# Two of ten row pairs are turned by VectorE after a trip over DRAM instead of by TensorE

## The chip, the cores and the metric

The program runs on one core of one Trainium2 chip. A core has five engines, each with its own in-order list of instructions: TensorE (PE in the profile, matmuls; PEld its weight loads), VectorE (DVE), ScalarE (ACT), GpSimd (POOL) and SyncE (SP, which here only issues transfers). Transfers run on 16 DMA engines. The metric is the device time of one execution in microseconds (us), lower is better; the median of several executions is given.

## The reference

One layer of graph attention over 2708 nodes with 1024 features, fp32, with a residual:

```python
h = jnp.maximum(_layernorm(x, axis=-1), 0.0)
q = h @ W_q.T + b_q
k = h @ W_k.T + b_k
v = h @ W_v.T + b_v
z = (1.0 / math.sqrt(1024)) * (q @ k.T)
spare_z = z * adj
spare_z = jnp.where(spare_z == 0.0, -10000.0, spare_z)
out = jax.nn.softmax(spare_z, axis=1) @ v
x = x + jnp.maximum(out, 0.0)
```

`adj` is a 0/1 matrix with a density of 0.15%, about four neighbours per row. x and adj are made by the seed; the weights are 1024x1024.

## The kernel before, in words

**What it computes.** The rows are sorted by their number of neighbours and cut into 22 tiles of 128. The scores of a row are products of one row of a transformed q with a few rows of h, and the result is a weighted sum of a few rows of h times the value weights; so there are two large products with a 1024x1024 matrix: the q products (h times a matrix made from W_q and W_k) and the o products (weighted rows times W_v). Between them lies the attention: for each tile, neighbours' rows of h are gathered, multiplied with the q row and summed (`junk<-g,pq`, L863), exponentiated (`w<-zall`, L872, on ScalarE), normed (L906 to L911) and added up with weights (`u<-g,coef`, L912 on ScalarE for the first neighbour, L923 on VectorE for the others).

**Units.** A unit is a pair of tiles. Units 0 to 9 are q pairs (tiles 0 and 1, 2 and 3, ...), units 10 to 18 are o pairs, and a single tile (`alone`) ends the program. Each unit is multiplied by a scheme with seven half-sized products instead of eight (`multiply` and `opened`): with a11, a12 the two halves of the first tile, a21, a22 of the second, s1 = a22 + a21, s3 = a11 - a21, s2 = s1 - a11 and s4 = a12 - s2. The products of unit n run on TensorE in the order s2, a12, s4, s3, then a11 and s1 of unit n+1, then a22 of unit n. Each is 8 records of 128x512 (L1011), in three PSUM banks (two named `ps`, one `psy`); ScalarE copies banks out (`u<-psy` L1060 after s2, `q<-ps` L1094 after a12, `taken<-psy` L1081 after s3, `psy<-ps` L1024 after a11, `p<-ps` L1029 after s1, `q<-psy` L1105 after a22) and fills new ones with the bias (`ps<-bp_sb` L760).

**Turning the rows.** TensorE wants its left operand with the features on the partitions. The rows of a q pair are gathered from `h_dram` into tiles named `qr` by GpSimd (L612). `half_turned` (L415) then makes 4 transposes of 128x128 on TensorE for each half tile into PSUM (`pt`; 8 records a half); ScalarE copies a11, a12 and a22 out (`a<-pt`, L718), and VectorE reads a21 from PSUM when it makes s1 and s3 (`put`, L722). Most o rows go another way: ScalarE writes a tile in an order of quarters (`v<-u`, L944), stores it to `u_dram`, SP reads it back with four transfers that put each quarter of the columns on its own 32 partitions (`by_quarters`, L700), and VectorE turns blocks of 32x32 (`faces`, L705), which then gives the same operand; `blocks` chooses by whether a tile is in `faced`.

**What sets the order.** In unit `FIRST` = 4 and after, VectorE's list is written by hand: the units' instructions come where the Python program emits them, and the attention runs as a stream (`attention`) that `advance(share)` moves on after each product by a number of microseconds of VectorE work. ScalarE, GpSimd, SP and TensorE are put in order by a scheduler that follows its own estimate of when each instruction's inputs are ready, with `issue_after` as a rule that one instruction comes after another in issue. The attention can start once the table of sorted neighbours has been written to DRAM by GpSimd (L626) and read back by SP (`tab`, L638 and L642). On ScalarE also stands `M<-M` (L1280), two halves that change the sign of a loaded part of W_v (t1, loaded at L1274 through SP), which the s1 products of the o units use.

## Time and profile before

| | us |
|---|---|
| median of 3 runs | 631.02 |
| lowest, highest | 630.44, 631.29 |
| profiled execution, whole | 627.16 |
| its span in the profile | 625.5 |
| TensorE busy | 618.3 (99%) |
| VectorE busy | 525.7 (84%) |
| ScalarE busy | 291.0 (47%) |
| GpSimd busy | 368.9 (59%) |

The profiled execution is one run; 1.66 us of it lie outside the span, and it is 3.86 us shorter than the median of the others. The granted TensorE clock is 0.997 of full speed. A row of a timeline has the start in us from the span's beginning, the duration, the engine, the line, the operation, the tiles (out<-in) and, in brackets, how long the engine stood idle before it and what ended that. A row of a group has the count, the busy time and the mean duration in ns. In a row of a stretch, each engine's busy time comes with its number of instructions, then the granted clock, the busy share of the DMA engines and GB/s.

### The profile page before, as it was taken

Reading aid. Unit: us, or ns where it says so; the run is one execution under the profiler, and the core shown is the slowest. Engines: PE = TensorE matmul, PEld = TensorE weight load, DVE = VectorE, ACT = ScalarE, POOL = GpSimd, SP = SyncE. Lnnn points to the kernel's source line nnn. Section 1 sums busy time; section 2 is a strip of 40 time slices with the busy share of each in tenths; the row PEclk is TensorE's granted clock in tenths of the full one; section 3 lists DMA queues with packets and bytes.
Section 4 is the critical chain, followed back from the end, with each engine's and each line's share of the span. In section 5 each row is a group of like instructions: output and inputs, shape, how many; then the busy total and the mean of one; then the engine's idle time right before and its main releaser. Section 6 shows DMA issues by size and latency. Waiting matters only on the chain.

```text
span 625.5 us, 6068 instructions
## 1 busy us (share of the span) xinstructions
PE 618.3 (99%) x1571; PEld 309.9 (50%) x1571; DVE 525.7 (84%) x1024; ACT 291.0 (47%) x421; POOL 368.9 (59%) x394
## 2 busy tenths in 40 slices
PE   9999999999999999999999999999999999999996
PEld 5777776444444444454444444444444444444442
DVE  5999878987988947979898999998988899898541
ACT  3538976749777373434331532443442433432300
POOL 2638870786668577856655343577577657752331
PEclk9999999999999999999999999999999999999998
DMA  8998898687797559997696999999999999995571
GB/s 336 407 374 318 332 352 326 211 273 292 267 370 277 175 180 364 342 347 233 218 362 170 397 340 313 339 326 320 328 328 320 333 306 338 288 301 144 137 266 71
DMA packets 65808, 183.24 MB, mean 293 GB/s; under 512 B 10039, under 2 KB 20615, under 8 KB 65128
## 3 DMA queue, kind: packets, MB, share of 16 engines
q0 software_dynamic: 26656, 86.02, 43.7%
q1 hardware_dynamic: 32170, 72.06, 33.0%
q10 hardware_dynamic: 6942, 24.73, 10.1%
q8 instruction: 14, 0.23, 0.1%
q14 instruction: 26, 0.21, 0.1%
HBM read 147.23 MB, written 43.88 MB: 306 GB/s over the span
## 4 chain that ended last, share of the span: by engine, by line
PE 90%; DMA 3%; POOL 2%; ACT 2%; DVE 1%; issue 0%; POOLq 0%; ACTq 0%
PE ps L1011 42%; PE psy L1011 30%; PE ps_y L476 7%; PE ps_x L476 4%; PE ps_z L476 4%; PE pt L415 2%; POOL hsum L298 2%; DMA x<-in_x_dram 2%; ACT sized L368 1%; DMA wlow<-in_wq_dram 1%; DVE wlow L444 1%; DVE s L722 0%; ACT junk_x L246 0%; PE ps_h L1230 0%; PE ps_v L594 0%
## 5 line engine op out<-in xcount | busy, mean ns | idle before, releaser
L610 POOL DMA_INDIRECT g<-h_dram,tab x93 | 120.5, 1296 | 62.4 <-issue 19.4
L1011 PE MATMUL psy<-wlow,s 128*128 128x512 f32 x320 | 144.0, 593 | 0.2 <-ACT u L1060 0.2
L1011 PE MATMUL ps<-M,a 128*128 128x512 f32 x320 | 144.1, 593 | 0.1
L863 DVE SCALAR_TENSOR_TENSOR junk<-g,pq 128x1024 uint8<-128x1024 f32 x92 | 112.3, 1220 | 9.3 <-DMA g<-h_dram,tab 7.3
L1011 PE MATMUL ps<-M,s 128*128 128x512 f32 x240 | 107.9, 592 | 0.0
L1011 PEld LDWEIGHTS ps<-M,a 128*128 128x128 f32 x320 | 60.0, 190 | 72.6 <-issue 71.5
L1011 PEld LDWEIGHTS psy<-wlow,s 128*128 128x128 f32 x320 | 60.0, 190 | 72.5 <-issue 71.3
L923 DVE SCALAR_TENSOR_TENSOR u<-g,coef,u 128x1024 f32<-128x1024 f32 x70 | 89.8, 1282 | 7.2 <-ACT u L912 5.4
L389 DVE FIND_INDEX8 at<-ones,adj 128x8 uint32<-128x685 f32 (+1 forms) x88 | 74.4, 863 | 0.0
L1011 PEld LDWEIGHTS ps<-M,s 128*128 128x128 f32 x240 | 45.5, 190 | 57.2 <-issue 55.5
L1011 PE MATMUL psy<-wlow,a 128*128 128x512 f32 x160 | 71.9, 592 | 0.0
L368 ACT ACTIVATE sized<-adj 128x2708 uint8<-128x2708 f32 (+1 forms) x22 | 54.3, 2468 | 7.5 <-DMA adj<-in_adj_dram 6.2
L298 POOL TENSOR_TENSOR hsum<-hsum,x 128x256 f32<-128x256 f32 (+1 forms) x56 | 38.6, 725 | 24.9 <-DVE wlow L444 21.5
L1115 POOL DMA_INDIRECT y<-in_x_dram,tab x19 | 33.2, 1749 | 31.4 <-ACT y L1132 16.6
L1011 PEld LDWEIGHTS psy<-wlow,a 128*128 128x128 f32 x160 | 30.4, 190 | 38.3 <-issue 36.6
L808 POOL DMA_INDIRECT out_dram<-y,tab x21 | 27.9, 1329 | 15.8 <-issue 13.6
L1011 PE MATMUL ps<-wlow,s 128*128 128x512 f32 x80 | 36.0, 593 | 0.0
L944 ACT COPY v<-u 128x1024 f32<-128x1024 f32 x20 | 20.9, 1046 | 29.9 <-DVE u L923 27.6
L912 ACT ACTIVATE u<-g,coef 128x1024 f32<-128x1024 f32 x16 | 18.4, 1148 | 25.7 <-DVE coef L911 20.5
L626 POOL DMA_INDIRECT tab_dram<-tab,pos_i x22 | 21.6, 982 | 14.3 <-DVE pos_i L689 8.8
L276 ACT ACTIVATE x<-x,r 128x1024 f32<-128x1024 f32 (+1 forms) x22 | 25.9, 1235 | 6.9 <-POOL r L266 6.9
L760 ACT COPY ps<-bp_sb 128x512 f32<-128x512 f32 x42 | 24.6, 596 | 8.7 <-DVE y L1150 7.2
(253 smaller groups left out, 839.1 us busy)
## 6 DMA issues: line engine op xcount, KB each, us to landing
adj<-in_adj_dram SPq DMA_DIRECT2D x21, 1354.0 KB, 11.4
x<-in_x_dram SPq DMA_DIRECT2D x21, 512.0 KB, 7.7
h_dram<-x ACTq DMA_DIRECT2D x21, 512.0 KB, 7.9
u_dram<-v ACTq DMA_DIRECT2D x20, 512.0 KB, 8.2
or<-u_dram SPq DMA_DIRECT2D x80, 128.0 KB, 7.9
q_late<-q SPq DMA_DIRECT2D x12, 512.0 KB, 8.5
pq<-q_late POOLq DMA_DIRECT2D x12, 512.0 KB, 9.3
M<-in_wv_dram SPq DMA_DIRECT2D x3, 1024.0 KB
```

The source lines that it names most:

```text
L276: nc.scalar.activation(xs[i][:n], xs[i][:n], AF.Relu, bias=r[:n, 4, i:i + 1], scale=r[:n, 3, i:i + 1])
L298: small.append(nc.gpsimd.tensor_add(hsum[:n, cols], hsum[:n, cols], xt[:n, cols]))
L368: nc.scalar.activation(sized[:n], a[:n, :, :PW], AF.Abs, accum_out=total[:n, t:t + 1])
L389: nc.vector.max_index(at[:n, k - first_k, g, :], ones[:n, 0:8], a[:n, g, :])
L476: mm = nc.tensor.matmul(bank, a_tile(o + H * a[0], a[1], i), b(o), start=first and o == 0, stop=(o == H - 1), skip_group_check=True)
L610: return nc.gpsimd.indirect_dma_start(out=dst, out_offset=None, in_=src, in_offset=off, bounds_check=N - 1, oob_is_err=False)
L760: nc.scalar.copy(return_[h], row[:, h * NB:(h + 1) * NB])
L808: to = nc.gpsimd.indirect_dma_start(out=out, out_offset=bass.IndirectOffsetOnAxis(ap=ptab.bitcast(U32)[:n, t, SLOTS:SLOTS + 1], axis=0), i ...
L863: chained(lambda: nc.vector.scalar_tensor_tensor(junk, g_of[t][s], 1.0, tq[t], op0=ALU.mult, op1=ALU.mult, accum_out=zall[:, t, s:s + 1]))
L923: chained(lambda: nc.vector.scalar_tensor_tensor(u, g_of[t][s], coef[:, s:s + 1], u, op0=ALU.mult, op1=ALU.add))
L1011: mm = nc.tensor.matmul(bank, a[:, c, :], b[:, c, :], start=False, stop=(c == 3), skip_group_check=True)
L1115: return nc.gpsimd.indirect_dma_start(out=y[:n], out_offset=None, in_=x, in_offset=off, compute_op=ALU.add)
```

## The change

The units 5 and 6 (`ROUND`; tiles 10 to 13) take for their q rows the way of the o rows. `send_round` copies each gathered tile in the order of quarters on ScalarE into a tile `way` and stores it to a new array `r_dram` (512 KB a tile, issued by ScalarE); `come_round` reads it back with `by_quarters` (four reads of 128 KB a tile, on SP) into `came`; `faces` turns the halves on VectorE. Their transposes on TensorE and the copies out of PSUM go. Round about:

- the reload of the table comes on SP after the last read of `came`, and is written in unit 4 after product 0 rather than 4;
- the store of q tile 8 comes on SP after the reload of the table, and so does the load of t1, now written in unit 4 rather than 7;
- the rows of unit 6 are gathered in unit 3 (at 4), earlier than before;
- unit 5's a11 and a12 are written two products later, together with the rest of the pair;
- the attention stream gets 2.3/7 us less after each product of unit 5, and one and a half shares at its start, after the last product of unit 4.

```diff
@@ steps of the stream
             elif step[0] == "b":
-                reload(*halves[first])
+                with tc.issue_after(came[-1].ins):
+                    tabbed.append(reload(*halves[first]))
@@ steps_at
-... (4, 4): "b0"}
+... (4, 0): "b0"}
@@ opened
         if n == FIRST:
             follow("o0")
+            send_round(ROUND[0])
@@ between
+        if n == FIRST - 1:
+            for m in ROUND[1:]:
+                send_round(m)
+            come_round(ROUND[0])
@@ q_results
-            (nc.scalar if t < 4 else nc.sync).dma_start(dst, q)
+            with tc.issue_after(tabbed[-1].ins) if t == EARLY else nullcontext():
+                stored.append((nc.scalar if t < 4 else nc.sync).dma_start(dst, q))
@@ new functions
+    ROUND = range(FIRST + 1, FIRST + 1 + 2)
+    came, tabbed, stored = [], [], []
+    def in_quarters(v, u):
+        return nc.scalar.copy(v.rearrange("p (a c r) -> p c a r", a=QUADS, r=QP),
+                              u.rearrange("p (c a r) -> p c a r", a=QUADS, r=QP))
+    def round_row(n, k):
+        t = 2 * (n - ROUND[0]) + k
+        return r_dram[t * P:(t + 1) * P, :]
+    def send_round(n):
+        for k, xt in enumerate(rows_of[n]):
+            v = row_tile(f"way_{n}_{k}")
+            in_quarters(v, xt)
+            nc.scalar.dma_start(round_row(n, k), v)
+    def come_round(n):
+        rows_of[n] = [row_tile(f"came_{n}_{k}") for k in range(2)]
+        for k, xt in enumerate(rows_of[n]):
+            came.append(by_quarters(xt, round_row(n, k)))
@@ the loop over units
+        if n > FIRST and n + 1 in ROUND:
+            share -= 2.3 / 7
@@ after
-            for at, place, src in (((-2, 0), t1, of_wv(0, 0)), ((0, 3), b21, of_wv(1, 0))):
-                if (n - last_q, i) == at:
-                    nc.sync.dma_start(place, src)
+            if (n - last_q, i) == (0, 3):
+                nc.sync.dma_start(b21, of_wv(1, 0))
             elif (n, i) == (FIRST, 6):
-                advance(share)
+                advance(1.5 * share)
                 if i == (3 if n == 0 else 4 if turn else 0):
                     ops_of[n + 1] = blocks(...)
-                    with tc.issue_after(products[-1].ins) if n + 1 == FIRST else nullcontext():
-                        ops_of[n + 1][1]()
+                    if n + 1 != ROUND[0]:
+                        with tc.issue_after(products[-1].ins) if n + 1 == FIRST else nullcontext():
+                            ops_of[n + 1][1]()
+                if i == (4 if n == 0 else 5 if turn else 2):
+                    if n + 1 == ROUND[0]:
                         ops_of[n + 1][1]()
-                if i == (4 if n == 0 else 5 if turn else 2):
                     ops_of[n + 1][2]()
+            if (n, i) == (FIRST - 1, 4):
+                rows_of[FIRST + 2] = load_rows(units[FIRST + 2])
+            if (n, i) == (FIRST - 1, 6):
+                with tc.issue_after(stored[-1].ins):
+                    come_round(FIRST + 2)
+            if (n, i) == (FIRST, 0):
+                with tc.issue_after(tabbed[-1].ins):
+                    tabbed.append(nc.sync.dma_start(t1, of_wv(0, 0)))
```

What the scheduler makes of it is seen in the order of instructions on the engines. First ScalarE, from the negation of t1 on; before, the exponential of the first attention tile (`w_1661`) stood three rows behind it, and the copy of unit 5's a12 result (its bank is `ps_1592`) comes eight rows after the last one shown:

```order
L1280 ACTIVATE M<-M 128x1024 x2
L1081 COPY taken<-psy 128x512
L1024 COPY psy<-ps_1592 128x512
L872 ACTIVATE w_1661<-zall 128x3
L1029 COPY p_1643<-ps_1594 128x512
L912 ACTIVATE u_1683<-g_1425,coef 128x1024
L872 ACTIVATE w_1704<-zall 128x3
L1105 COPY q_1534<-psy 128x512
```

The same place now, where the bank of unit 5's a12 result is `ps_1609` and the first exponential `w_1674`:

```order
L1089 COPY taken<-psy 128x512
L1027 COPY psy<-ps_1609 128x512
L1033 COPY p_1658<-ps_1611 128x512
L1114 COPY q_1571<-psy 128x512
L763 COPY ps_1755<-bp_sb 128x512
L1103 COPY q_1678<-ps_1609 128x512
L763 COPY ps_1757<-bp_sb 128x512
L1314 ACTIVATE M<-M 128x1024 x2
L875 ACTIVATE w_1674<-zall 128x3
L915 ACTIVATE u_1684<-g_1430,coef 128x1024
L875 ACTIVATE w_1709<-zall 128x3
L1068 COPY u_1717<-psy 128x512
```

The first exponential has moved behind the copies of unit 5's a11, s1 and a12 results, and the negation from ahead of `taken` to just ahead of it; the copy `u_1717<-psy` of unit 5's s2 result stands behind the second exponential.

VectorE before, from the weights of the first attention tile to the first sum of unit 6 (`s_1731` is its s1, `pt` the transposed a21):

```order
L906 SCALAR_TENSOR_TENSOR w_1661,m_1681<-w_1661,keys 128x3
L910 RECIPROCAL m_1681<-m_1681 128x1
L911 TENSOR_SCALAR coef<-w_1661,m_1681 128x3
L863 SCALAR_TENSOR_TENSOR junk_1688,zall<-g_1430,pq_1613 128x1024
L923 SCALAR_TENSOR_TENSOR u_1683<-g_1426,coef,u_1683 128x1024
L923 SCALAR_TENSOR_TENSOR u_1683<-g_1427,coef,u_1683 128x1024
L863 SCALAR_TENSOR_TENSOR junk_1717,zall<-g_1431,pq_1690 128x1024
L722 TENSOR_TENSOR s_1731<-a_1724,pt 128x512
```

And now, up to where the sums of unit 6 follow (`a_1691` is its a11, `a_1726` its a22):

```order
L909 SCALAR_TENSOR_TENSOR w_1674,m_1682<-w_1674,keys 128x3
L913 RECIPROCAL m_1682<-m_1682 128x1
L914 TENSOR_SCALAR coef<-w_1674,m_1682 128x3
L866 SCALAR_TENSOR_TENSOR junk_1689,zall<-g_1435,pq_1628 128x1024
L708 STREAM_TRANSPOSE a_1691<-came_0_1522 128x4x4x32
L708 STREAM_TRANSPOSE a_1693<-came_0_1522 128x4x4x32
L926 SCALAR_TENSOR_TENSOR u_1684<-g_1431,coef,u_1684 128x1024
L926 SCALAR_TENSOR_TENSOR u_1684<-g_1432,coef,u_1684 128x1024
L866 SCALAR_TENSOR_TENSOR junk_1722,zall<-g_1436,pq_1695 128x1024
L866 SCALAR_TENSOR_TENSOR junk_1724,zall<-g_1437,pq_1695 128x1024
L708 STREAM_TRANSPOSE a_1726<-came_1_1523 128x4x4x32
L708 STREAM_TRANSPOSE s_1728<-came_1_1523 128x4x4x32
```

The turns of unit 6's first tile stand behind the first weights and one score, those of its second behind two sums and two more scores. On TensorE, one of the four parts of a11 of unit 6 (`a_1691`) now stands ahead of s3 of unit 5:

```order
L1014 MATMUL ps_1611<-M,s_1602 128x512 x4
L1014 MATMUL ps_1755<-M,a_1691 128x512
L1014 MATMUL psy<-wlow,s_1595 128x512 x4
L1014 MATMUL ps_1755<-M,a_1691 128x512 x3
L1014 MATMUL ps_1757<-wlow,s_1730 128x512 x4
```

Before, the four parts of a11 followed s3 in one row; each part is two of the records of L1011.

6 lines of the change are left out of this document (4 added, 2 removed), and 2 rows, old and new, of the table steps_at.

## The prediction

> **What bounds the kernel now.** I read the page's first part, then its chain of waits, then the timeline of TensorE around the units that the change touches.
>
> ```profile
> PE 618.3 (99%) x1571; PEld 309.9 (50%) x1571; DVE 525.7 (84%) x1024; ACT 291.0 (47%) x421; POOL 368.9 (59%) x394
> PE 90%; DMA 3%; POOL 2%; ACT 2%; DVE 1%; issue 0%; POOLq 0%; ACTq 0%
> L415 PE MATMUL pt<-ident,qr x96: 272/273/273, 201.1 to 325.0; 128*128 128x128 f32 x96
> 232.26 3.60 PE L1011 MATMUL ps<-M,a 128*128 128x512 f32 x8
> 239.12 3.60 PE L1011 MATMUL psy<-wlow,a 128*128 128x512 f32 x8
> 242.56 1.04 PE L415 MATMUL pt<-ident,qr 128*128 128x128 f32 x8
> 243.43 3.60 PE L1011 MATMUL psy<-wlow,s 128*128 128x512 f32 x8
> 246.87 1.04 PE L415 MATMUL pt<-ident,qr 128*128 128x128 f32 x8
> 247.74 3.60 PE L1011 MATMUL ps<-M,a 128*128 128x512 f32 x8
> 251.18 3.60 PE L1011 MATMUL ps<-M,s 128*128 128x512 f32 x8
> 258.04 3.60 PE L1011 MATMUL ps<-M,a 128*128 128x512 f32 x8
> 261.48 1.88 PE L1011 MATMUL ps<-wlow,s 128*128 128x512 f32 x4
> ```
>
> TensorE is busy for 618.3 us of 625.5 and carries 90% of the chain; in this stretch one product (8 matmuls) starts 3.43 us after the last, with no hole. Of the products, 232.26 is a11 of pair 5, 251.18 its s4 (its s3 follows), 258.04 a11 of pair 6, 261.48 its s1. So a TensorE instruction that goes is worth its whole length, and one that waits costs its whole wait. All else counts only where TensorE comes to wait for it.
>
> **What is removed.** Each group of 8 transposes takes 243.43 - 242.56 = 0.87 us out of TensorE's row, and 247.74 - 246.87 = 0.87 again. The change removes four such groups (two of pair 5, two of pair 6): 4 x 0.87 = 3.5 us. The program has 12 groups of this kind (x96); 8 stay. ScalarE also loses six copies of what was turned, off the path.
>
> [...]
>
> **What is added, and what hides it.** VectorE gets 8 block turns, ScalarE 4 reordering copies and 4 stores, SP 16 reads of 128 KB.
>
> ```profile
> L705 DVE STREAM_TRANSPOSE a<-or x29: 660/704/708, 347.3 to 573.6; 128x512 f32<-128x512 f32 x29
> L944 ACT COPY v<-u 128x1024 f32<-128x1024 f32 x20 | 20.9, 1046 | 29.9 <-DVE u L923 27.6
> L700 SPq DMA_DIRECT2D or<-u_dram x80: 302/431/1187, 321.2 to 592.3; - x80
> DMA to landing us min/median/max: 3.1/7.9/15.6
> qr<-h_dram,tab POOLq DMA_INDIRECT x5, 5.3
> 207.56 0.93 POOL L612 DMA_INDIRECT qr<-h_dram,tab  x1 [0.30 <-issue]
> 210.00:225.00 15.00, 15.00 (x49) 7.49 (x48) 12.08 (x21) 9.11 (x18) 8.82 (x13) 1.00 0.27 89
> 221.43 0.91 DVE L1270 MEMSET g<- 128x1024 f32 x1 [0.16 <-issue]
> 225.16 0.38 SPq L638 DMA_DIRECT2D tab<-tab_dram  x1
> 238.31 1.23 DVE L863 SCALAR_TENSOR_TENSOR junk<-g,pq 128x1024 uint8<-128x1024 f32 x1 [3.18 <-DMA g<-h_dram,tab]
> ```
>
> Pairs 5 and 6: the last of their four gathers is issued at 207.56 and lands some 5.3 us later, so by 212.9 all rows are there, pair 5's earlier. Pair 5 at the latest: copy 1.05 to 214, a store of some 3 to 4 us (the DMA engines are 27% busy between 210 and 225, so landings near the minimum of 3.1), four reads of 0.43 us issue each and their landing: 222 to 223, when VectorE finishes its memsets at 221.43 + 0.91 = 222.3. Four turns of 0.70 and the sums end near 228; a11 of pair 5 is wanted at 232.26 - 1.75 = 230.5. Cost nothing, cover some 5 to 7 us; beyond that it would cost one for one. Pair 6 follows 3 us behind. The table load that stands behind its reads on SP (225.16) may move by 0 to 1.5 us, and 1 MB of reads more can delay the first gathers by about 3; attention's first score (238.31) then moves by 0 to 4.5 us. The tile-8 store and the t1 load stand after the table load before and after the change.
>
> **The wait that the order makes.** Here I expect the saving to go. Until now the exponential of the first attention tile (`w<-zall`) stands on ScalarE ahead of the copies of pair 5's s1, s2 and a12 results; now it stands behind the copy of a12's result, a bias copy and the two-part negation `M<-M`. ScalarE takes its list strictly in turn:
>
> ```profile
> 231.71 2.00 ACT L1280 ACTIVATE M<-M 128x1024 f32<-128x1024 f32 x2 [3.45 <-DMA M<-in_wv_dram]
> 242.14 0.20 ACT L872 ACTIVATE w<-zall 128x3 f32<-128x3 f32 x1 [5.67 <-DVE junk L863]
> 242.25 0.57 ACT L1029 COPY p<-ps 128x512 f32<-128x512 f32 x1
> 224.57 0.62 ACT L760 COPY ps<-bp_sb 128x512 f32<-128x512 f32 x1
> 225.08 1.08 ACT L375 ACTIVATE junk_m<-M 128x1024 uint8<-128x1024 f32 x1
> 245.30 1.15 ACT L912 ACTIVATE u<-g,coef 128x1024 f32<-128x1024 f32 x1 [2.48 <-issue]
> 244.56 0.19 DVE L906 SCALAR_TENSOR_TENSOR w<-w,keys 128x3 f32<-128x3 f32 x1
> 245.12 1.22 DVE L863 SCALAR_TENSOR_TENSOR junk<-g,pq 128x1024 uint8<-128x1024 f32 x1
> 246.48 2.60 DVE L923 SCALAR_TENSOR_TENSOR u<-g,coef,u 128x1024 f32<-128x1024 f32 x2
> 252.89 0.69 DVE L722 TENSOR_TENSOR s<-s,a 128x512 f32<-128x512 f32 x1
> ```
>
> The copy `p<-ps` shows it: its product had ended by 239.12, yet it ran at 242.25, behind the `w` that waited 5.67 us. [...] If ScalarE could let `w` overtake, the sum would be the whole 3.5 us; that case is rival A.
>
> Now the times, with all four groups gone: s4 of pair 5 starts at 251.18 - 3.50 = 247.68, so a12's result can be read at about 247.85. Then on ScalarE two copies of 128x512, 0.5 each (225.08 - 224.57 from one start to the next), the negation 1.9 to 2.0, and `w` 0.2: 250.9. VectorE has its fifth score done at 244.6 (plus 0 to 4.5, which this hides) and stands still up to 6.4 us. From `w`: weights 0.56 (245.12 - 244.56), a score 1.26, then the first turn of pair 6, 0.70: a11 ready at 253.5. TensorE's list asks for a quarter of it at 247.68 + 3.43 = 251.1, ahead of s3. Stall 2.4 us. The s3 behind it also needs the copy `u<-psy`, which on ScalarE comes after the tile's first weighted row (1.15) and the second `w`, about 253.5 too; the two waits overlap.
>
> Next, VectorE does the second turn, two sums (2.5), two scores (2.5), two turns (1.35) and s1's addition (0.7): s1 ready at 253.5 + 0.7 + 2.5 + 2.5 + 1.35 + 0.7 = 261.2 at the most; where the pitches are shorter than the durations, 261.0. TensorE gets there after two products: 253.5 + 6.87 = 260.4. Stall 0.7. Sum: -3.5 + 2.4 + 0.7 = -0.4 us. Both stalls are sums of rows with an error of perhaps 0.3 each. If neither came the sum is -3.5; with s1's only, -2.8.
>
> **VectorE is late afterwards.** It has lost 6.4 us and 2.8 us (four turns), against 0.55 + 0.81 of idle that it had here anyway: about 7.7 us late at pair 6. Does that come out at TensorE later?
>
> ```profile
> 270.93 1.23 DVE L863 SCALAR_TENSOR_TENSOR junk<-g,pq 128x1024 uint8<-128x1024 f32 x1 [3.53 <-DMA g<-h_dram,tab]
> 259.31 1.69 POOL L610 DMA_INDIRECT g<-h_dram,tab  x1 [0.30 <-ACT w L872]
> 382.21 0.69 DVE L722 TENSOR_TENSOR s<-a,s 128x512 f32<-128x512 f32 x1
> 388.61 3.60 PE L1011 MATMUL ps<-M,s 128*128 128x512 f32 x8
> DVE p L1127 <- ACT taken L1081: 4.2, 4, 1.6
> DVE u L1131 <- PE ps L1011: 2.9, 3, 1.4
> 598.20 1.25 DVE L705 STREAM_TRANSPOSE T_alone<-or 128x1024 f32<-128x1024 f32 x1 [10.62 <-DMA or<-u_dram]
> 602.36 1.88 PE L1011 MATMUL ps<-M,T_alone 128*128 128x512 f32 x4
> ```
>
> The score at 270.93 waited 3.53 us for a gather issued at 259.31, 11.6 us earlier. Now it waits for a slot that ScalarE frees with its first weighted row of the second tile: pair 6's sums until 263.1, weights 0.56, the row 1.15, so 264.8, and lands near 264.8 + 11.6 = 276.4. VectorE arrives at 270.93 - 3.53 + 7.7 = 275.1 and waits 1.3 instead of 3.5: 2.2 us are taken up, 5.5 remain. At unit 11 (s1 ready 382.9, wanted 388.61: 5.7 us of room) one score fewer (1.3) lies ahead of it in VectorE's list, so 4.2 us late: no stall. After that the waits for TensorE's results (4.2 + 2.9 us, 406 to 571) take up the rest. The single tile's turn ends at 599.45 and is wanted at 602.36: 2.9 us of room. I put the later loss at zero, bounds 0 and 3.5.
>
> Span 625.5 - 0.4 = 625.1, profiled run 627.16 - 0.4 = 626.8; that run lies 3.9 us under the median of the runs, 631.02, so on their scale **630.6 us**.
>
> **The rivals.**
> A. The whole saving, 631.02 - 3.5 = 627.5. For it: TensorE saves this for certain, and only my reading of two lists stands against it. It holds if `w` is done before 248.5, or if pair 6's turns don't wait for it. Against: VectorE's list has the turns behind `w`'s consumer. The price without `w`'s wait but with VectorE's own load is between the two.
> B. Slower: VectorE's lateness isn't taken up. If the gathers slip as far as VectorE does, 7.7 - 1.3 = 6.4 us reach unit 11 (room 5.7, stall 0.7) and, if the waits for TensorE's results don't absorb it either, the single tile: T_alone then comes 2 to 3.5 us after its place. With 5 us left at the end it costs 5 - 2.9 = 2.1, and with unit 11's share -0.4 + 0.7 + 2.1 = +2.4: 633.4. It decides from a lateness of about 4.2 us at the end on. For it: VectorE is 84% busy over the span, and hardly idle but for the listed waits from unit 6 to 16; against: 7.1 us of waits tied to TensorE.
> C. Slower: the way over DRAM is late, pair 5's operands after 230.5 or the table load by over 6 us; 2 us beyond the cover end at +1.6, 632.6. For it: landings reach 15.6 us under load. Against: 27% busy there.
> D. Faster, in part: only one of the two stalls comes, s1's (-2.8, 628.2) or a11's (-1.1, 629.9), because `w` or the turns come about a microsecond sooner than my sum has them. For it: each stall is a small difference of long sums.
>
> **How the numbers follow.** About 1.26 us (0.2%) is what a measurement here can tell from no change: faster is under 629.76, slower over 632.28. My forecast has 0.47, its own range 629.5 to 632.0 (0.3 per stall and up to 1 us of later waits): faster 0.06, same 0.39, slower 0.02. A has 0.13, all faster; D 0.12, faster 0.09 and same 0.03; B 0.20 and C 0.08 are slower with 0.27, same with 0.01. Sum: faster 0.28, same 0.43, slower 0.29. The range is 627.5, A's time, to 633.4, B's.
>
> **What would show it.** In the changed profile: transposes of gathered q rows x64; s4 of pair 5 some 3.5 us earlier; `w<-zall` on ScalarE behind an `M<-M` near 249 to 251; an idle of 5 to 6.5 us ahead of VectorE's first weights row; a TensorE wait of 2 to 3 us at a11 of pair 6 and under 1.2 us at its s1; s1 of pair 6 near 261 as before. I am wrong if TensorE runs through there (A), if its idle time lies at 230 (C), or if a wait appears at unit 11 or at the single tile (B).

## The result, and the profile after

The changed kernel took **635.21 us** (median of 9 runs, 634.79 to 636.88). The kernel before, on the same chip, took 630.18 us (9 runs, 628.75 to 634.20). The ratio is **1.0081 (95% interval 1.0063 to 1.0099)**: slower by 5 us. I had predicted 630.6 us with a range up to 633.4, so the time lies outside it.

The profiled execution took 636.88 us with a span of 635.1, that is 1.7 us above the median; the one of before lay 3.0 us below the median of its 9 runs. The two spans therefore differ by 9.6 us where the medians differ by 5.0, and part of what follows is that. First the part of the page with the busy times and the engines' shares of the chain of waits, after:

```profile
PE 620.0 (98%) x1539; PEld 308.0 (48%) x1539; DVE 531.0 (84%) x1032; ACT 292.8 (46%) x419; POOL 368.2 (58%) x394
PE 40%; DVE 8%; issue 5%; DMA 3%; POOL 1%; ACT 1%; POOLq 0%; DVEq 0%; ACTq 0%
```

TensorE has 32 instructions fewer (1539 against 1571), as it should, and is yet busy for longer: some of them ran at a lower clock (0.50 of full speed from 204.12 to 207.54 and from 258.74 to 262.15). Followed back from the end, the chain breaks off at 269 us, so that its shares add up to 58% of the span; TensorE has 40 of these 58, where it had 90 of 98. What TensorE now waits for (us in total, times, longest):

```profile
PE psy L1014 <- DVE u L926: 2.7, 1, 2.7
PE ps L1014 <- ACT u L1068: 2.4, 1, 2.4
PE pt L417 <- DMA qr<-h_dram,tab: 2.1, 1, 2.1
```

Before there was no such wait in this part of the program. The places stand in TensorE's timeline after:

```profile
203.94 1.78 PE L417 MATMUL pt<-ident,qr 128*128 128x128 f32 x8 [2.09 <-DMA qr<-h_dram,tab]
...
252.21 3.60 PE L1014 MATMUL ps<-M,s 128*128 128x512 f32 x8
258.21 1.53 PE L1014 MATMUL ps<-M,a 128*128 128x512 f32 x2 [2.41 <-ACT u L1068]
259.54 4.90 PE L1014 MATMUL psy<-wlow,s 128*128 128x512 f32 x8
264.27 2.74 PE L1014 MATMUL ps<-M,a 128*128 128x512 f32 x6
266.85 3.60 PE L1014 MATMUL ps<-wlow,s 128*128 128x512 f32 x8
...
318.73 3.60 PE L1014 MATMUL ps<-wlow,s 128*128 128x512 f32 x8
325.06 3.70 PE L1014 MATMUL psy<-wlow,a 128*128 128x512 f32 x8 [2.73 <-DVE u L926]
```

252.21 is s4 of pair 5, 258.21 the first quarter of a11 of pair 6, 259.54 s3 of pair 5, 266.85 s1 of pair 6, 325.06 a22 of unit 7. I set each start against the start of the same product before (251.18 for s4 of pair 5, 261.48 for s1 of pair 6, 316.48 for a22 of unit 7). That gives the account of the 9.6 us (the lag is how much later a product starts than the same one before; 0.3 us come after the last row):

| place | what happens | lag behind the kernel before |
|---|---|---|
| 150 | | +0.37 |
| 204 to 211 | pair 4's rows land late, then a slow stretch | +4.54 |
| 217 to 252 | four groups of transposes are gone, 3.51 | +1.03 |
| 258 to 267 | wait at a11 of pair 6 (2.57 behind the place it would have had), then a slow stretch (1.77) | +5.37 |
| 325 | 0.3 on the way, then the wait at a22 of unit 7 | +8.58 |
| 377 | wait at a22 of unit 9 | +9.26 |

The saving came in full. The first of the losses has to do with the executions at least in part: that wait for pair 4's rows lies ahead of all that the change touches on TensorE. It stands in all ten profiles of the changed kernel and its variants (1.0 to 2.7 us), and in four of the ten profiles of the kernel before and of its variants (1.2 to 3.4 us; 1.23 in the second profile of before, below). Whether the change makes it more frequent is not shown. Without it the account is 0.37 - 3.51 + 4.34 + 3.21 + 0.68 = **5.1 us**. That this meets the difference of the medians is no proof, since the profiles are single executions, and in one without that wait the later losses need not be the same.

The wait at pair 6 is the one that I forecast, and its cause is seen on ScalarE, after:

```profile
252.41 0.58 ACT L1103 COPY q<-ps 128x512 f32<-128x512 f32 x1 [5.66 <-PE ps L1014]
253.02 0.59 ACT L763 COPY ps<-bp_sb 128x512 f32<-128x512 f32 x1
253.55 2.00 ACT L1314 ACTIVATE M<-M 128x1024 f32<-128x1024 f32 x2
255.45 0.19 ACT L875 ACTIVATE w<-zall 128x3 f32<-128x3 f32 x1
```

The exponential's three scores were done at 249.93, and it ran at 255.45, behind the copy and the negation. But on VectorE it is not the whole story. Its rows after, first the attention's first score, the first weights and the first turn of pair 6, then the end of unit 7:

```profile
246.14 1.23 DVE L866 SCALAR_TENSOR_TENSOR junk<-g,pq 128x1024 uint8<-128x1024 f32 x1 [8.94 <-DMA g<-h_dram,tab]
...
255.67 0.16 DVE L909 SCALAR_TENSOR_TENSOR w<-w,keys 128x3 f32<-128x3 f32 x1 [1.48 <-ACT w L875]
...
257.36 1.30 DVE L708 STREAM_TRANSPOSE a<-came 128x512 f32<-128x512 f32 x2
...
323.12 1.28 DVE L926 SCALAR_TENSOR_TENSOR u<-g,w,u 128x1024 f32<-128x1024 f32 x1 [2.08 <-ACT u L892]
324.33 0.68 DVE L1106 TENSOR_TENSOR q<-psy,p 128x512 f32<-128x512 f32 x1
```

The first score comes at 246.14 instead of 238.31, and VectorE's idle time lies ahead of it (8.94 us), not ahead of the weights (1.48 instead of the 5 to 6.5 that I expected). Not all of these 7.8 us belong to the change. The table is made from a small product of TensorE, which the lag of pair 4's place has moved as well, before and after:

```profile
209.73 0.23 PE L678 MATMUL ps_in<-sort,before 128*128 128x144 bf16 x1
214.26 0.23 PE L680 MATMUL ps_in<-sort,before 128*128 128x144 bf16 x1
```

From that product on (below: from `ps_in`), the first score comes after 31.9 us instead of 28.6, so 3.3 us later; 4.5 us are the lag.

And a22 of unit 7 waits until VectorE has read the bank that it writes into (`q<-psy,p`, done at 325.01; the brackets name the row ahead of it, done at 324.40, but TensorE starts at 325.06). In the kernel before, VectorE's row and TensorE's row for the same pair of instructions were

```profile
314.21 0.68 DVE L1097 TENSOR_TENSOR q<-psy,p 128x512 f32<-128x512 f32 x1
```

```profile
316.48 3.60 PE L1011 MATMUL psy<-wlow,a 128*128 128x512 f32 x8
```

that is done at 314.89 and wanted at 316.48: 1.6 us of room. I had looked for room at unit 11 and at the single tile, and not here.

Why the attention starts late is seen on SP, whose list holds the table's reload behind the trip's sixteen reads (the first eight take 6.63 us there, the last eight 3.40), and then on GpSimd, whose first gather waits for the table:

```profile
220.77 6.63 SPq L702 DMA_DIRECT2D came<-r_dram  x8
...
228.78 3.40 SPq L702 DMA_DIRECT2D came<-r_dram  x8
232.50 0.39 SPq L640 DMA_DIRECT2D tab<-tab_dram  x1
```

```profile
237.62 0.99 POOL L614 DMA_INDIRECT pq<-q_dram,tab  x1 [7.21 <-DMA tab<-tab_dram]
```

The reload is 7.3 us later than before (225.16), and 2.8 us later when it is measured from `ps_in` (18.2 instead of 15.4), where I had allowed 0 to 1.5. So two theories stand against each other: **the order on ScalarE** (the predicted stall and what follows from it are the loss) and **the late start of the attention** (the trip's transfers delay it, VectorE then runs late through all q units, and the loss appears wherever TensorE first needs VectorE's result).

### The profile page after: what moved, and what is told of

Its sections match the earlier page's. It is cut to its first block, busy times and chain, and to the rows that moved or that the text cites. A ratio compares the mean times of both kernels' runs of the same rounds, so it can differ in the third digit from the quotient of the medians.

```text
span 635.1 us, 6045 instructions
## 1 busy us (share of the span) xinstructions
PE 620.0 (98%) x1539; PEld 308.0 (48%) x1539; DVE 531.0 (84%) x1032; ACT 292.8 (46%) x419; POOL 368.2 (58%) x394
## 4 chain that ended last, share of the span: by engine, by line
PE 40%; DVE 8%; issue 5%; DMA 3%; POOL 1%; ACT 1%; POOLq 0%; DVEq 0%; ACTq 0%
PE ps L1014 23%; PE psy L1014 17%; DVE u L926 3%; DMA g<-h_dram,tab 3%; DVE junk L866 2%; DVE s L725 1%; POOL g L612 1%; DVE wlow L1319 0%; DVE q L1106 0%; DVE a L708 0%; DVE q L1109 0%; ACT u L915 0%; ACT u L892 0%; POOL M L1315 0%; POOL pq L614 0%
## 5 line engine op out<-in xcount | busy, mean ns | idle before, releaser
L1014 PE MATMUL psy<-wlow,s 128*128 128x512 f32 x320 | 146.3, 600 | 0.3 <-ACT u L1068 0.3
L1014 PEld LDWEIGHTS psy<-wlow,s 128*128 128x128 f32 x320 | 61.3, 194 | 75.3 <-issue 73.9
L811 POOL DMA_INDIRECT out_dram<-y,tab x21 | 25.7, 1224 | 15.9 <-issue 13.9
```

The source lines that it names most:

```text
L811: to = nc.gpsimd.indirect_dma_start(out=out, out_offset=bass.IndirectOffsetOnAxis(ap=ptab.bitcast(U32)[:n, t, SLOTS:SLOTS + 1], axis=0), i ...
L1014: mm = nc.tensor.matmul(bank, a[:, c, :], b[:, c, :], start=False, stop=(c == 3), skip_group_check=True)
```

## The experiments

Lines and names are those of the changed kernel unless the text says "before". Ratios are to the kernel before, which ran beside each group at medians of 629.65 to 629.70 us for the first twelve runs, 627.31 for the three that split the trip, 627.52 and 630.30 for the last ones.

### The kernel before, once more

To see how much one profile differs from the next.

> The kernel before, unchanged, for a second profile. All five profiles of changed kernels show a wait of TensorE of 1.7 to 2.7 us near 203 us for the gathered rows of pair 4, ahead of everything that the change touches, and in four of five a slow stretch behind it; the first profile of before does not, and its execution of 627.2 us is shorter than all of 19 timed ones (628.2 to 631.5). If the wait belongs to the kernel before as well, it stands in this profile, 1.5 to 2.7 us, with a span of about 627.5 to 630. If the change causes it, this profile has none and a span near 625.5.

It took 628.32 us, with a span of 626.6. The products stand as in the first profile, but pair 4's first transposes waited 1.23 us for their rows; the table's reload is at 225.85 and the first score at 239.32. From `ps_in` (210.83) these are 15.0 and 28.5 us, as in the first profile (15.4 and 28.6), so this distance leaves out what an execution has lost before.

### The order on ScalarE

`neg_later` holds the negation back behind the last exponential that the program has written by that place, so that it falls into unit 7 and no longer stands ahead of the first one (`exps` collects the exponentials):

```diff
+                    with tc.issue_after(exps[-1].ins):
                         nc.scalar.activation(t1[:, 2 * h:2 * h + 2], ..., AF.Copy, scale=-1.0)
```

> The change with one edit: the negation of t1 (M<-M, two halves, 1.9 us on ScalarE) is kept behind a later exponential, in unit 7, so that the first exponential comes 1.9 us sooner; nothing else moves near it. In the changed kernel TensorE stood still 2.57 us at a11 of pair 6 and then ran slowly (two stretches of 0.87 and 3.43 us took 1.33 and 4.73), 4.3 us in all, and again 2.7 us at a22 of unit 7, where it waits for VectorE's addition q<-psy,p. Theory T1 (VectorE, late since the first exponential, sets the pace: TensorE is pulled back to it at a22 of unit 7 and 9 whatever it won before): VectorE wins only its own wait of 1.5 us for that exponential, so the time falls by 1.5 us against the change, to about 633.7 where before is 630.2, and the stall at a22 of unit 7 grows from 2.7 to about 5. Theory T2 (the stalls stand by themselves and add up): the first loss falls by 1.9 us or, with the slow stretch, by 3.7, the later ones stay: 631.5 to 633.3, the stall at a22 of unit 7 still about 2.7.

633.04 us, ratio 1.0046 (1.0023 to 1.0070): 2 us better than the change, still 3 us slower than before. The wait at pair 6 didn't go, it grew (waits of TensorE and, on VectorE, the first score):

```profile
PE ps L1015 <- ACT u L1069: 4.9, 1, 4.9
PE psy L1015 <- DVE q L1107: 1.3, 2, 1.1
```

```profile
247.88 1.23 DVE L866 SCALAR_TENSOR_TENSOR junk<-g,pq 128x1024 uint8<-128x1024 f32 x1 [10.17 <-issue]
```

The first exponential now ran as soon as its scores were there (252.91, after scores from 247.88 on), and pair 6's turns were late all the same. In this build the scores bound pair 6, not the order on ScalarE. It isn't a clean test of that order, since the first score also came later, 36.5 us after `ps_in` instead of 31.9 in the change. In the change itself the two lay close together: the fifth score was done at 254.2, and the weights waited 1.48 us more for the exponential.

`taken_4_7` lets ScalarE copy s3's result out of its bank in units 4 to 7 (before, and in the change, only in 4 and 5), so that a22 no longer waits for VectorE there:

```diff
-... copied(Y) if EARLY <= ta < EARLY + 4 else Y ...
+... copied(Y) if EARLY <= ta < EARLY + 8 else Y ...
```

> The change with one edit: in units 6 and 7 as well ScalarE copies the result of s3 out of PSUM (taken), as it already does in units 4 and 5, so that a22 no longer waits for VectorE's addition there; the order is otherwise that of the change. T1 (VectorE is late as a whole): TensorE runs through a22 of unit 7, but meets VectorE again at a22 of unit 8 or 9, or at s1 of unit 9 to 11; the 2.7 us move there and the time falls by at most 0.5 us: 634.7 to 635.2 where before is 630.2. T2 (only this one wait binds): the 2.7 us and what slowness follows are gone, 632 to 632.5.

636.86 us, ratio 1.0108 (1.0084 to 1.0132): no gain. Unit 7's wait is gone, and the same wait stands at the next units that have no copy, 8 and 9 (1.47 us at 348.86, 2.16 at 375.32):

```profile
PE psy L1014 <- DVE q L1106: 3.6, 2, 2.2
```

(The wait at pair 6, whose order is that of the change, was 3.59 us here.) VectorE's lateness is carried on; removing the place where it shows moves it.

### Moving the table, the load, the turns

`table_first` puts the table's reload on SP ahead of pair 6's eight reads.

```diff
-            if (n, i) == (FIRST - 1, 6):
-                with tc.issue_after(stored[-1].ins):
-                    come_round(FIRST + 2)
...
             if (n, i) == (FIRST, 0):
+                with tc.issue_after(tabbed[-1].ins):
+                    come_round(FIRST + 2)
```

> The change with one edit: the reads of pair 6 from r_dram come on SP after the reload of the table instead of ahead of it. The reload was issued at 232.5 in the changed kernel, 2.8 us later than the start of its units explains, and landed 2 us slower. In this build the scheduler also puts the first exponential ahead of a12's copy and the negation behind. T1 (VectorE's lateness is made up of the late start of the attention and the wait for the exponential): the attention starts 3 to 5 us sooner, the first stall goes or falls under 1 us, and a22 of unit 7 waits under 1 us: the time falls to 626.7 to 630 where before is 630.2. Rival (the 5.6 us of additional turns and other work on VectorE alone keep it late): a22 of unit 7 still waits over 2 us, 632 or more.

636.46 us, ratio 1.0102 (1.0078 to 1.0125). The reload comes at 229.32 instead of 232.50, but the first score only at 245.93: it still waits 10.0 us for its gathers. The first one is issued at 235.50, right behind pair 6's reads (230.5 to 234.4), and its score comes 10.4 us later, where it took 6.0 in the change. TensorE waits 1.45 at s1 of pair 6, 2.6 at unit 7 and 1.2 at unit 6.

`t1_load_later` is `neg_later` with the load of t1 (1 MB), which stood right behind the table, written three units later; SP issues it at 243.96 instead of 233.96:

> As neg_later (633.0 us), with one edit more: the load of t1 (1 MB) is kept behind two stores of q rows on SP, out of the stretch in which the first gathers of the attention land. T3 (transfers set the attention's start, some 3 us a MB): first score 2 to 3 us sooner than in neg_later (there 247.9), the stall at pair 6 falls from 4.9 to about 2 us, 630 to 631. Rival (the start is set by the order of issue on SP and GpSimd and by latency, not by bytes): first score unchanged, 633.

633.89 us, ratio 1.0057 (1.0039 to 1.0076), as `neg_later`; the wait at pair 6 is 5.4 us. The first score did come 2.9 us sooner (245.03), but the fourth then waited 4.54 us for its gather. So moving that load out of the first gathers changes which gather is late, and not the time.

`pair_5_only` sends only pair 5 round (`ROUND` of one unit, and the earlier gathering of unit 6 left out):

> The change for unit 5 alone: two tiles go over r_dram (1 MB stored, 1 MB read) and unit 6's rows are gathered at their old time and turned by TensorE; 16 of the 32 transposes stay, so 1.75 us is what TensorE can save. Theory T3 (the attention's start is set by the transfers ahead of it: pair 6's reads on SP's list ahead of the table, and 1 MB more at some 340 GB/s among the first gathers): the table is read as soon as it is written, the first score comes within 2 us of its place in before, no stall of TensorE over 0.5 us follows: 628.0 to 628.5 where before is 629.7. Rival T1 (ScalarE's order alone makes the wait): in this build the exponential stands ahead of a12's copy too, so the same time; they differ in where the first score is. Rival (a way over DRAM costs what it saves, at whatever size): 629.7 or more.

635.03 us, ratio 1.0074 (1.0050 to 1.0097). Half the trip, half the saving, and nearly the same loss: the table at 229.74, the first score at 244.89, no wait at pair 6, but 5.6 us in two waits at a22 of units 6 and 7, and 2.1 for ScalarE's `u` at 283.58.

```profile
PE psy L1014 <- DVE q L1106: 5.6, 2, 2.8
```

`pair_6_in_the_gap` uses the time in which VectorE waits for its first gather: pair 6 is turned and added up there (all but s4), ScalarE's copies of s3 go on through all q units, the exponential goes ahead of a12's copy, and t1 is loaded as in `t1_load_later`:

```diff
             elif (n, i) == (FIRST, 6):
+                ops_of[FIRST + 2] = blocks(*rows_of[FIRST + 2], None)
+                ops_of[FIRST + 2][1]()
+                ops_of[FIRST + 2][2](False)
                 advance(1.5 * share)
```

> t1_load_later, and: pair 6 is turned and summed (but for s4) ahead of the first score, in the 9 us in which VectorE waits for the first gathers; the first exponential and the copy of s2's result stand ahead of a12's copy; ScalarE copies s3's result in all q units from 4 on. TensorE then waits for nothing of the attention at pair 6. If T3 and VectorE's lateness are the whole story: no stall over 0.5 us after 220 us, the 3.5 us are saved: 626.2 to 627.5 where before is 629.7. Rival (VectorE's lateness comes out at a later place, s1 of units 9 to 11 or the single tile): 628 to 630.

633.13 us, ratio 1.0049 (1.0020 to 1.0078). No wait at pair 6, as meant; the lateness comes out at pair 7 (1.50 us for its gathered rows, 1.84 for VectorE's s1) and at 366.93 (2.73).

`all_eased` takes the reliefs together: table first, the exponential ahead of a12's copy, the negation later, pair 6's first tile turned ahead of unit 5's share of attention, ScalarE's copies of s3 in all q units from 4 on.

> All edits together: the table ahead of pair 6's reads, the first exponential ahead of a12's copy, the negation later, a11 and a12 of pair 6 turned before the first weights, and ScalarE copies s3's result in all q units from 4 on. T1: no stall of TensorE over 0.5 us between 230 and 400 us, the whole 3.5 us saved: about 627 where before is 630.2. Rival (ScalarE's added copies or VectorE's lateness come out further on, at s1 of unit 11 or at the single tile): 628.5 to 631.

631.82 us, ratio 1.0030 (1.0014 to 1.0046): the best version with pairs 5 and 6 on the trip, and still slower than the kernel before. One wait of VectorE's making is left (1.92 us at s1 of pair 6).

`turned_before_scores` goes one step further from there and makes all of pair 6's operands but s4 ahead of unit 5's share:

> As all_eased (631.8 us, whose one stall is 1.9 us and a slow stretch at s1 of pair 6), with all of pair 6's operands but s4 made ahead of unit 5's share of the attention. The stall at s1 goes. T4 (a lateness of 5 us or more has to come out somewhere): TensorE then waits at another place, between units 7 and 11, for 2 us or more: 630.5 to 633. Rival (that stall was the last one): 627.5 to 628.5.

634.80 us, ratio 1.0082 (1.0055 to 1.0110). At pair 6 TensorE then had the whole saving (3.4 us ahead of `before_again`'s place); after it came waits for pair 7's rows (2.71 at 270.39), for ScalarE's copy of s3 (0.98) and for a part of W_v (2.04 at 367.97). What was gained at one place was given back at the next.

`paced` is `turned_before_scores` with 1.5 us less for the attention in each of units 5 to 9 and 0.8 more in each o unit, so that the q units aren't late:

```diff
+        if FIRST < n <= last_q:
+            share -= 1.5 / 7
+        elif n > last_q:
+            share += 0.8 / 7
```

> As turned_before_scores, with the attention's share after each product cut by 1.5/7 us in units 5 to 9 (7.5 us in all) and raised by 0.8/7 in the o units, so that VectorE's list does TensorE's work earlier and lets the attention lag, to be caught up where VectorE waits for TensorE (7 us from 406 to 571). T4: no stall of TensorE up to unit 11; if the lag is caught up by the end, 626.5 to 628 where before is 629.7; if it is not, it comes out at the single tile, where there were 2.9 us of room: 629 to 632.

641.22 us, ratio 1.0169 (1.0128 to 1.0210). The lateness isn't made up: it comes out at the end, with waits of 2.7 us at 592 and 2.9 us for the single tile. The longest wait, 3.3 us at 275, is again for the gathered rows of pair 7.

### The late start alone

None of these versions had removed the loss. The next ones leave the change out: they are the kernel before with one part of the trip's side effects.

`before_table_late` only puts the table's reload behind the store of q tile 8 on SP:

```diff
+                with tc.issue_after(stored[-1].ins):
-                reload(*halves[first])
+                    reload(*halves[first])
```

> The kernel before with one edit: SP issues the reload of the table behind the store of q tile 8 (near 230 us) instead of at 226, so that the attention starts some 4 to 5 us later; nothing of the round trip, all transposes on TensorE. Theory T4 (what costs is the late start of the attention: VectorE has no room to catch up, and TensorE is made to wait for it at the places where it needs VectorE, plus a slow stretch behind a long wait): first score 4 to 5 us later, and of that 2 to 5 us come out at TensorE: 631.5 to 634.5 where before is 629.7. Rival (the change's loss comes from its added VectorE work, its own reads or ScalarE's order, and a start 4 us late is caught up before it matters): 629.3 to 630.5.

635.00 us, ratio **1.0082 (1.0055 to 1.0110)**, the ratio of the change itself, without any turn, trip or saving. SP, VectorE and TensorE in it:

```profile
231.78 0.38 SPq L639 DMA_DIRECT2D tab<-tab_dram  x1
```

```profile
245.25 1.23 DVE L864 SCALAR_TENSOR_TENSOR junk<-g,pq 128x1024 uint8<-128x1024 f32 x1 [9.88 <-DMA g<-h_dram,tab]
```

```profile
296.43 5.40 PE L1012 MATMUL psy<-wlow,a 128*128 128x512 f32 x8 [4.19 <-DVE q L1098]
```

Six microseconds of delay at the first score (34.2 after `ps_in` instead of 28.5) make a22 of unit 6 wait 4.19 us for VectorE, fifty microseconds later, and the product after the wait takes 5.40 instead of 3.60. Here ScalarE's order costs nothing: the negation stays ahead, at 229.54, the first exponential stands behind some more copies but runs when its scores are there, at 249.06, and the weights follow the fifth score without a wait. (The store and the load of t1 now stand ahead of the table on SP.)

`before_plus_traffic` adds copies from DRAM to DRAM that stand for the trip (4 of 512 KB on ScalarE's queue, 16 of 128 KB on SP ahead of the table) and changes no computation:

> The kernel before with the transfers of the trip and nothing else of it: ScalarE issues four copies of 512 KB from h_dram to r_dram where the change stores its tiles, SP sixteen of 128 KB ahead of the table (behind the last store of the early q tiles, and here also the store of tile 8). VectorE, ScalarE and TensorE compute as before. T4 with the trip's transfers as the reason of the late start: first score 4 to 8 us later than in before (239), 632 to 636. Rival (the trip's bytes fit into the idle stretch of the DMA engines; only SP's waiting for the stores to land delays the table): first score within 2 us, 629.5 to 631.

634.82 us, ratio **1.0088 (1.0055 to 1.0122)**: the transfers alone lose 5.5 us without any saving. The change loses 5.0 on balance, so some 8.5 ahead of its saving of 3.5; the transfers account for 5.5 of that, and not for all. They do more than delay the table (reload at 234.28, first score 35.1 us after `ps_in`): the scheduler answered with a new order on ScalarE, as in the change, with the negation and then the first exponential (256.38) behind the copy of a12's result.

### Which part of the trip

Three more, with parts of that traffic. `before_stores_only` has the four copies on ScalarE's queue, `before_reads_only` the sixteen on SP ahead of the table's reload. `before_reads_behind` has the sixteen right behind it; although its expectation says no stores, its edit holds the four copies on ScalarE's queue too:

```diff
# stores only
+            for t in range(4):
+                nc.scalar.dma_start(r_dram[t * P:(t + 1) * P, :], h_dram[t * P:(t + 1) * P, :])
# reads only: 16 times, the reload behind the last one; reads behind: the reload first
+                    nc.sync.dma_start(r_dram[4 * P + 32 * t:4 * P + 32 * t + 32, :], h_dram[...])
```

> The kernel before with only the four 512 KB copies that stand for the trip's stores, on ScalarE's queue; nothing on SP. If the stores cost the start of the attention by themselves (they hold up the scattered writes of the table and the q rows of tile 8): last write of the table near 227, first score 243 to 245 instead of 239.3, and 632 to 634 us. If it is the reads on SP ahead of the table that count: first score 239 to 241, and 629 to 631 us.

627.09 us, ratio 1.0003 (0.9993 to 1.0013): the stores cost nothing. SP's reload and VectorE's first score come no later than before:

```profile
223.81 0.38 SPq L639 DMA_DIRECT2D tab<-tab_dram  x1
```

```profile
237.00 1.23 DVE L864 SCALAR_TENSOR_TENSOR junk<-g,pq 128x1024 uint8<-128x1024 f32 x1 [3.47 <-DMA g<-h_dram,tab]
```

> The kernel before with only the sixteen 128 KB copies on SP ahead of the table's reload. If the reads on SP are the cause: the table's load 4 to 7 us later (230 to 233 instead of 225.9), first score 244 to 247, and 633 to 635 us. If the stores are: first score under 242, and 629 to 631 us.

632.45 us, ratio **1.0074 (1.0057 to 1.0091)**. SP, VectorE and TensorE:

```profile
217.77 11.16 SPq L1327 DMA_DIRECT2D r_dram<-h_dram  x16
230.22 0.39 SPq L640 DMA_DIRECT2D tab<-tab_dram  x1
```

```profile
243.22 1.23 DVE L865 SCALAR_TENSOR_TENSOR junk<-g,pq 128x1024 uint8<-128x1024 f32 x1 [9.41 <-DMA g<-h_dram,tab]
```

```profile
295.39 5.40 PE L1013 MATMUL psy<-wlow,a 128*128 128x512 f32 x8 [2.81 <-DVE q L1099]
```

And ScalarE's negation, with VectorE's first weights:

```profile
253.94 2.00 ACT L1283 ACTIVATE M<-M 128x1024 f32<-128x1024 f32 x2 [1.55 <-DMA M<-in_wv_dram]
...
256.07 0.16 DVE L908 SCALAR_TENSOR_TENSOR w<-w,keys 128x3 f32<-128x3 f32 x1 [4.76 <-ACT w L874]
```

Sixteen issues of 0.70 us each hold SP for 11.2 us; the table comes 6.4 us later than with the stores only, the first score 6.2. But here too the scheduler put the first exponential behind the negation, whose load slipped on SP from 224.93 to 243.55, and VectorE waits 4.76 us more for it. So this run has both theories in it, the late start and the order on ScalarE. (The real reads take (6.63 + 3.40) / 16 = 0.63 us each.)

> The kernel before with the same sixteen copies on SP right behind the table's reload instead of ahead of it, and no stores. If SP's list alone counts: table at 226, first score 239 to 241, 629 to 631 us. If the copies also slow the first gathers, which they now meet: table at 226, but first score 243 to 245 and 632 to 634 us.

632.08 us, ratio **1.0074 (1.0057 to 1.0091)**, the same loss with the table in time and the first exponential ahead of the negation. VectorE and TensorE:

```profile
239.86 1.23 DVE L867 SCALAR_TENSOR_TENSOR junk<-g,pq 128x1024 uint8<-128x1024 f32 x1 [6.25 <-DMA g<-h_dram,tab]
```

```profile
289.43 3.70 PE L1015 MATMUL ps<-wlow,s 128*128 128x512 f32 x8 [2.22 <-ACT ps L764]
295.07 3.70 PE L1015 MATMUL psy<-wlow,a 128*128 128x512 f32 x8 [1.93 <-DVE q L1103]
```

The first gather of neighbours was issued at 229.76 here and at 229.49 with the stores only; its score comes 10.1 us after it instead of 7.5. Besides, t1's load slips on SP from 224.9 to 250.0. So the reads cost in two ways: as a block on SP's list (11.2 us in `before_reads_only`), and, behind the table, in a first gather that takes 2.6 us longer; moving them past the table exchanges one for the other. That they slow this gather as load on the DMA engines is my estimate and was not shown: the engines' busy share was 0.80 from 225 to 235 us and 1.03 from 235 to 245, and with the stores only 0.89 and 0.97. That fits `table_first`, which gained nothing. The stores, which alone cost nothing, are in this run as well; what they cost together with the reads, and what the late load of t1 costs, was not separated.

### The same trip elsewhere

Is it the place, or has VectorE no room for a q pair's turns anywhere? `trip_of_pair_9` is the kernel before in which only unit 9 goes round, its rows gathered 60 us after the attention's start; the attention gets 2.3 us less in unit 8. `trip_of_pairs_8_9` does it for two.

```diff
+        if n + 1 in ROUND:
+            share -= 2.3 / 7
...
                     rows_of[n + 2] = load_rows(units[n + 2])
+                    if n + 2 in ROUND:
+                        trip(n + 2)
```

> The kernel before in which only unit 9, long after the attention's start, takes the trip over DRAM: rows gathered near 295 to 305, turned before 331; the attention's share is 2.3 us less in unit 8. If the loss of the change comes from the place (the trip's reads at the attention's start): first score stays at 239 to 240, two groups of transposes go, TensorE saves 1.7 us, and VectorE's 2.8 us more come out at most at the single tile (room 2.9), so ratio 0.997 to 1.000. If VectorE has no room for turns anywhere in units 5 to 9: waits of TensorE for VectorE's q of units 8 and 9, and 1.002 to 1.006.

626.85 us, ratio 0.9986 (0.9976 to 0.9995). VectorE turns pair 9 between two shares of attention with no idle time ahead of it, and TensorE's only new wait is 0.2 us at the single tile; first VectorE, then the waits:

```profile
321.26 1.30 DVE L706 STREAM_TRANSPOSE a<-came 128x512 f32<-128x512 f32 x2
327.40 0.71 DVE L706 STREAM_TRANSPOSE a<-came 128x512 f32<-128x512 f32 x1
```

```profile
PE ps L1012 <- DVE T_alone L706: 0.2, 1, 0.2
```

TensorE's lead grows by 1.75 us where the two groups went. Of it 0.87 is lost again at 516.67: the kernel's own rule, which turns an o tile on VectorE only if the tile is done in time, sent one more tile to TensorE, since the attention was later.

> The same for units 8 and 9: TensorE saves 3.5 us, VectorE gets 5.5 us more, of which the stream must give back 4.6 in units 7 and 8 and 2 to 3 us more than its room at the end. Place theory: 0.996 to 1.001. No-room theory: waits for VectorE's q of units 7 to 9, 1.002 to 1.008.

637.09 us, ratio 1.0139 (1.0112 to 1.0165). Not the wait that either theory had named: ScalarE's copy into quarter order waits for its gathered rows, and behind it in ScalarE's list stand a result's copy and the bias for TensorE's next bank. ScalarE, then TensorE:

```profile
285.84 1.04 ACT L1226 COPY way<-qr 128x1024 f32<-128x1024 f32 x1 [6.64 <-DMA qr<-h_dram,tab]
...
288.92 1.04 ACT L1226 COPY way<-qr 128x1024 f32<-128x1024 f32 x1 [2.03 <-DMA pq<-q_late]
```

```profile
291.12 6.74 PE L1012 MATMUL ps<-wlow,s 128*128 128x512 f32 x8 [3.46 <-ACT ps L761]
```

Two more waits follow, 2.99 us at 374.66 for ScalarE's `psy` and 1.47 at the single tile. So this run says nothing on VectorE's room at unit 8; it shows the price of a reordering copy that the scheduler places before its data are there.

`pair_9_smaller_cut` is `trip_of_pair_9` with 1.2 instead of 2.3, so that the o tile stays on VectorE:

> The kernel before with only unit 9 on the trip, as in trip_of_pair_9, but the attention's share in unit 8 is cut by 1.2 us instead of 2.3, so that no further o tile falls back to TensorE (there one did, 0.87 us). If the tail has no more room than trip_of_pair_9 showed (its single tile already waited 0.2 us): the 0.87 us come back at the single tile as a wait of 0.5 to 1.5 us, ratio 0.997 to 0.999. If the smaller cut also brings the single tile forward: no wait there, ratio 0.996 to 0.998.

630.04 us, ratio 0.9996 (0.9980 to 1.0012): no difference to before that can be measured. Its profile has the wait for pair 4's rows at its largest (3.36 us at 204.85), which hides what would have shown at the single tile, so that part of the expectation stays open. The one new wait is 0.77 us for VectorE's `q` at 372.60.

## Why the prediction was wrong, point by point

**TensorE is the bound, and each group is worth 0.87 us: right.** 3.51 us came, group by group.

**Pair 5 is in time: right.** Its turns ran from 229.12 to 231.85 and a11 was wanted at 235.04. The trip itself wasn't late for TensorE, so the first of rival C's two forms didn't happen.

**The stall at a11 of pair 6: right in size, incomplete in price.** Predicted 2.4, measured 2.41 (2.57 behind the ideal place), with `w` behind the negation and the tile's first weighted row ahead of `u<-psy`, as worked out: `w` came 3.24 us after the start of s4, where I had 3.2. But the stall was followed by a stretch at half clock that cost 1.77 us more, which no row of the kernel before could show. The second stall (0.7 at s1) didn't come, since the slow stretch made TensorE late: s1 was ready at 265.6, TensorE arrived at 266.85, and without the stretch it would have arrived at 265.1. Sum of this place: predicted +3.1, measured +4.34.

**"I put the later loss at zero": wrong, and this is the step that failed.** The loss after pair 6 was 3.9 us (3.21 up to a22 of unit 7, 0.68 up to unit 9). I looked for room where VectorE makes TensorE's operands (s1 of unit 11, 5.7 us; the single tile, 2.9 us), and not where VectorE frees the bank that TensorE writes next: a22 waits for `q<-psy,p`, and unit 7 had 1.6 us. Against a lateness of 5.5 us, which I had worked out myself, that decides; the row stood in the profile of before. Measured, `q<-psy,p` was 10.1 us later than before (324.33 against 314.21), 5.6 without the 4.5 of pair 4's place, so the lateness itself was as forecast. (The four terms that I gave for it, 6.4 + 2.8 - 0.55 - 0.81, make 7.8 at pair 6 and not 7.7, which changes nothing.) Together with the slow stretch, +1.77, which stood in no term, this is the loss that the sum lacks.

**"Attention's first score then moves by 0 to 4.5 us", "which this hides": right up to the weights in the profiled execution, and partly by luck.** The score moved by 3.3 us from `ps_in` on, inside the range, and VectorE still waited 1.48 us for `w`. But the range had the wrong terms. I had allowed the reload 0 to 1.5 us, and it moved by 2.8; no row stood behind "1 MB of reads more" and "about 3". The sixteen reads take 10 us in SP's list and hold it, with a q tile's store between them, from 220.8 to 232.2: the last eight took the 0.43 us each that I had worked with, the first eight twice that, and I had not added them up against the place of the reload. In the nine variants the first score came 4 to 8 us later from `ps_in` on, so in most of them the attention's start was near the end of the range or beyond it, and in `neg_later` the scores held up pair 6, not the exponential.

**The rivals.** What happened is B's mechanism, VectorE's lateness coming out later, at another place than B named. B's time, 633.4, was too low because it counted only what exceeds the rooms at unit 11 and at the single tile, and had no slow stretch. C's cause, the transfers ahead of the table, was at work too, but moved the reload by 2.8 us from `ps_in` on, less than C's 6. Two things made VectorE late in the change, the order on ScalarE and the late start of the attention. By the rows at the first weights, which came 6.6 us later (without the 4.5), either alone would have left most of it: without the order 1.5 us would have gone, without the late start nothing. This is read from one profile and not tested. That a late start alone suffices for such a loss is shown by `before_table_late` (+0.82%), where ScalarE's order made no wait. That the reads suffice is shown by `before_reads_only` (+0.74%), but by way of both. No run has ScalarE's new order alone, so its share is open; easing it in `neg_later` took the loss from 0.81% to 0.46%, with intervals that just overlap. That a q pair's turns on VectorE and TensorE's saving need not cost anything is shown for one pair by `trip_of_pair_9`, which does not lose. Open is also what the same trip would do at unit 8 with the copy placed behind ScalarE's other work, and whether the gain for pair 9 is real: 0.9986 and 0.9996 with overlapping intervals allow a tenth of a per cent or nothing.

## What to carry to other kernels

Where an engine will run late, list every instruction by which it frees something (a bank, a slot) for the bound engine, beside those by which it makes operands, and take the smallest room of all; the rooms of before can be read row against row. Look at a transfer that is added first for what stands behind it in its issuing engine's list: here the small load that starts a whole stage, the table's, came 6.4 us later behind sixteen reads, and where it was put ahead of reads, the score of the stage's first gather came 10.4 us after it instead of 6.0 (`table_first`) and 10.1 instead of 7.5 (`before_reads_behind`). When removing a stall only moves it, reproduce the suspected cause in the kernel before, without the change: `before_table_late` showed here what nine variants of the change had not. Then compare the order on every engine with the kernel before; in two of the other such runs the scheduler had changed a second thing along with the one that was meant.

## What the runs showed of the hardware

A wait of TensorE cost more than its length in some cases here: the granted clock was at half afterwards, 0.50 for 3.41 us behind the wait at pair 6. In these views of stretches of the changed kernel, TensorE's clock stands ahead of the DMA share; the first two rows are the two slow stretches, the third starts with the wait's end at pair 6, the last with that at unit 7:

```profile
204.12:207.54 3.42, 3.42 (x11) 2.38 (x10) 3.11 (x17) 1.17 (x2) 3.42 (x6) 0.50 0.45 180
258.74:262.15 3.41, 3.41 (x6) 1.34 (x5) 3.38 (x3) 0.94 (x1) 2.69 (x3) 0.50 0.82 287
258.21:263.21 5.00, 5.00 (x8) 2.19 (x9) 4.93 (x6) 1.04 (x1) 3.78 (x5) 0.66 0.87 304
325.06:330.06 5.00, 5.00 (x18) 2.79 (x19) 4.89 (x4) 1.26 (x3) 3.78 (x5) 1.00 1.01 404
```

A mean of 0.66 over 5 us loses 5 x 0.34 = 1.7 us, as measured (1.77). But after the longer wait at 325.06 (2.73 us) the clock stayed full (1.00). Over all profiles of this case I took every wait of TensorE above 0.7 us from 150 us on and the mean clock of the 5 us after it:

| wait | number | followed by a mean clock of 0.71 or less |
|---|---|---|
| 0.77 to 1.87 us | 21 | 0 |
| 1.91 to 3.27 us | 25 | 12 |
| 3.36 to 5.39 us | 6 | 6 |

So here the 21 waits of up to 1.87 us cost their length (the mean clock after each was 1.00), and the six of 3.36 us and more cost 1.5 to 3 us more (an estimate from the clock after them: 0.71 over 5 us loses 1.5; the largest, 3.0, is 0.50 over 5 us and 0.89 over the next 5). What decides between them was not shown. In the changed kernel's profile a pattern can be read from where the slow stretches start: at 204.12, 258.74 and, when the products have ended, 634.20. These lie 16 and 110 whole steps of 3.413 us apart, the length of each of the first two. Cut at the borders of such steps, the waits of 2.09 and 2.41 us ahead of the first two stretches lie within one step each, and the wait at 325.06 is cut into 1.26 and 1.48 us. So in these three half clock came where 2 us or more of the wait fell into one step, and not where 1.48 did. They are three waits of one profile, read afterwards; no run moved a wait on purpose.
